# Reordering the start of a vision tower and the turn of its last image

## The chip, the cores and the metric

The kernel runs on one core of a Trainium2 chip. The metric is the device time of one execution, in microseconds (us); the kernel before has a median of 746.74 us over three runs (746.47 to 747.71). One further execution was recorded by the hardware profiler, and every row of a profile below is from such an execution. Engines are named as the profile names them: PE (matrix multiplication), DVE (VectorE), ACT (ScalarE), POOL (GpSimd) and SP (which here only starts transfers). Each engine runs its own queue of instructions in order and waits on semaphores for the others.

## The reference, cut to what matters

Four images of 3 x 224 x 224 pixels go through a tokenizer and two layers, all in float32. The tokenizer normalises 8 x 8 patches (192 values), multiplies them by `W1`, normalises, multiplies by `Wp1`, normalises, applies SiLU and multiplies by `Wp2`:

```python
tokens = layernorm(patches, ln1_g, ln1_b) @ W1 + b1
tokens = layernorm(tokens, ln2_g, ln2_b)
tokens = jnp.concatenate([tokens, tokens, tokens], axis=1)
h1 = silu(layernorm(tokens @ Wp1 + bp1, lnp_g, lnp_b))
return h1 @ Wp2 + bp2
```

Layer 0 is an attention *between the images* at each place, with a gate, and a mixture of six experts of which each token takes two:

```python
att = softmax(einsum('slhc,tlhc->sth', q, k) * scale, axis=1)
o = einsum('sth,tlhc->slhc', att, v) * sigmoid(mn @ Wg + bg)
...
top_w, top_i = top_k(softmax(relu(x @ router_w1 + b) @ router_w2 + b), 2)
out = sum over the two chosen experts of weight * expert(x)
```

Layer 1 is a linear attention and a small mixture of four experts. Tokens are repeated three times, so only a third of the rows is computed and the result is written three times.

## The kernel before, in words

Each image has 784 rows: six tiles of 128 rows and 16 rows left over; the leftovers of the four images share one more tile.

**Start.** SP and ACT issue the loads of the first weights and of the pixels (nine transfers into `img`). POOL issues the bias `bp1` and thirteen small vectors into `stage` (46 rows of 128 values) early. `first_layers` (L361) folds the first weight matrices into `Wall`; it is a generator whose parts are interleaved by hand with the pixels' work: `flatten(k)` (L341) copies the pixels of a seventh of the patches into rows, on DVE or ACT; `turn_patches(k, c)` (L349) transposes four columns of patches on PE (`ptp`) and copies them out to `pT`; `patch_stats` and `patch_stds` (L446, L451) find the standard deviations. At the end `stage` is transposed on PE to the columns `cols` (L525, L526). Large buffers in DRAM, `xrows` and `yrows`, are cleared by 46 transfers from a tile of zeros, `nothing`, behind that last copy. POOL also fills constant tables (`base0`, `table`, `blk`, `shift`).

**Middle.** `tokenize` works through groups of tiles; its order is left to the scheduler. From `turn_second(0)` on, the order of PE, DVE and ACT is written by hand (`tc.manual_schedule`): what stands earlier in the code stands earlier in each engine's queue. Keys and values of all images are computed (`keys_values`), and then each image s takes its turn (`added_rows`, `weighed`): `products` (DVE) multiplies queries with the keys of each image, `shares_before` and `shares_after` make the softmax `att`, `gate_mm` and `gate_act` the gate, `first_value` and `values` the weighted sum `oT`, `attended` multiplies by `Wo` (`pwo`), adds to `h` and takes the sums of squares, `rows_of_part` normalises, `turn_part` transposes (`pt`) to `xT`, `router` (`pr`, `rT`) and `router_logits` (`plg`) make the router's logits, `choose` (18 small DVE instructions) picks two experts, `count` (`pcount`) numbers the rows, and `send` computes their places and has POOL scatter them to `xrows`, one transfer for each tile and choice.

**Expert blocks.** Rows are handled in blocks of 256 of one expert. `early_blocks` (L1171) makes the list of the first seven blocks from the first two images, in three steps that alternate PE and DVE. A block is loaded by SP (`load`), transposed on PE (`turned`: `ptb`, `xTb`), its expert's weights are copied to one place by DVE (`own_weights`, which first reads the expert's offset from the list into a register), and then multiplied three times (`hidden(i, 0)`, `hidden(i, 1)`: `pb`, `hb`; `rows_back`: `pyb`, `yb`). The last image's turn (L1517 on) is interleaved by hand with the first blocks. All the experts' weights, `ew`, take the place of the keys and queries, `kq`, and are loaded by six transfers of SP once the last product has been taken; the loads of the first four blocks stand behind these on SP.

After the blocks, layer 1 follows; the change does not touch it.

Of the kernel before, what the change touches and what calls it, by code (L numbers as in the profile page):

```python
# [27 lines left out]
P = 128  # L28
TT = 128
# [43 lines left out]
def tile_vit_tower(ctx: ExitStack, tc: tile.TileContext, a: dict, out: bass.AP):  # L73
# [97 lines left out]
    img = tokp.tile([IP, CY, WID], F32, tag="img", name="img")  # L171
    bp1 = tokp.tile([TT, D], F32, tag="bp1", name="bp1")
    nc.gpsimd.dma_start(out=bp1, in_=a["L0_tok_bp1"].partition_broadcast(TT))
# [3 lines left out]
    for src, n, width in plan:  # L177
        nc.gpsimd.dma_start(out=stage[r0 : r0 + n, :width], in_=src)
        r0 += n
# [154 lines left out]
    pL = tokp.tile([P, 2, NI, SEG], F32, tag="pL", name="pL")  # L334
    nc.gpsimd.memset(pL, 1.0)
# [4 lines left out]

    def flatten(k, put):  # L341
        put(
            flat[:, k * PW : (k + 1) * PW, :PD].rearrange("q w (y x) -> q w y x", x=PATCH),
            img[:, :, k * PW * PATCH : (k + 1) * PW * PATCH].rearrange(
                "q y (w x) -> q w y x", x=PATCH
            ),
        )

# [12 lines left out]
    def first_layers():  # L361
# [68 lines left out]
        nc.vector.tensor_copy(Wall[:, :, D:], pp)  # L430
# [41 lines left out]
    with tc.manual_schedule(engines=by_hand):  # L472
        nc.vector.memset(srow, 0.0)
        nc.vector.memset(srow[:, SROW : SROW + 1], 1.0)
        nc.vector.memset(perm, 0.0)
        nc.vector.memset(perm[:, :, :PD], -1.0 / PD)
        by_y = ident[:KP, :KP].rearrange("p (y x c) -> p c y x", x=PATCH, c=CH)
        for half in range(2):
            nc.vector.tensor_scalar(
                perm[:, half, :PD].rearrange("p (c y x) -> p c y x", c=CH, x=PATCH)[  # L480
                    :, :, 4 * half : 4 * (half + 1)
                ],
                by_y, -1.0 / PD, None, ALU.add,
            )
        nc.scalar.activation(root_, one_, AF.Sqrt, bias=one_)
        warm = ps_tile("pwarm")
        for _ in range(6):
            nc.tensor.transpose(warm[:, :P], ident, ident)
        steps = first_layers()
        next(steps)  # L490
        NK = HP // PW
        cut0 = 5
        flatten(0, nc.vector.tensor_copy)
        flatten(1, nc.scalar.copy)
        turn_patches(0, 0)
        for k in range(2):
            patch_stats(k)
        flatten(3, nc.vector.tensor_copy)
        flatten(2, nc.scalar.copy)
        turn_patches(1, 0)  # L500
        next(steps)
        for k in range(2, cut0):
            patch_stats(k)
        turn_patches(2, 0)
        flatten(4, nc.scalar.copy)
        next(steps)
        turn_patches(3, 0)
        flatten(5, nc.scalar.copy)
        turn_patches(4, 0)
        patch_stds(0, cut0)  # L510
        turn_patches(5, 0)
        flatten(6, nc.scalar.copy)
        for k in range(2):
            turn_patches(k, 1)
        turn_patches(6, 0)
        for k in range(cut0, NK):
            patch_stats(k)
        for k in range(2, cut0):
            turn_patches(k, 1)
        patch_stds(cut0, NK)  # L520
        next(steps)
        turn_patches(5, 1)
        turn_patches(6, 1, nc.vector.tensor_copy)
        pc = ps_tile("pc")
        nc.tensor.transpose(pc[:, :nrows], stage, ident[:nrows, :nrows])  # L525
        turned = nc.vector.tensor_copy(cols, pc[:, :nrows])  # L526

# [16 lines left out]
    rb2 = spread(wts, "rb2", a["L0_ffn_router_b2"])  # L544
    for put in weight_loads:
        tc.add_manual_dep(
            put.ins, arrived[0],
            mybir.DependencyInfo(mybir.DependencyClass.Sync, mybir.DependencyReason.DATA),
            reason="behind the images",
        )  # L550

    nothing = tokp.tile([P, 7 * D], F32, tag="nothing", name="nothing")
    nc.gpsimd.memset(nothing, 0.0)
    for r in range(0, XROWS, 7 * P):
        n = min(7, (XROWS - r) // P)
        for rows_ in (xrows, yrows):
            put = nc.sync.dma_start(
                out=rows_[r : r + n * P, :].rearrange("(p k) d -> p (k d)", k=n),
                in_=nothing[:, : n * D],
            )  # L560
            tc.add_manual_dep(
                put.ins, turned.ins.name,
                mybir.DependencyInfo(mybir.DependencyClass.Sync, mybir.DependencyReason.DATA),
                reason="later",
            )
# [7 lines left out]
    base0 = const.tile([TT, E0], F32, tag="base0", name="base0")  # L573
    for e in range(E0):
        nc.gpsimd.memset(base0[:, e : e + 1], float(CAP * e))


    NQ = QMAX * E0
    table = const.tile([1, 5, NQ], F32, tag="table", name="table")
    for q in range(QMAX):  # L580
        nc.gpsimd.memset(table[:, 0, q * E0 : (q + 1) * E0], float(BLK * q))
    by_e = table.rearrange("r k (q e) -> r k q e", e=E0)
    for e in range(E0):
        for k, v in (
            (1, CAP * e - DUMMY), (2, EW * e), (3, D * e), (4, CAP * e - DUMMY + SMALL)
        ):
            nc.gpsimd.memset(by_e[:, k, :, e], float(v))
    for k in (1, 4):
        nc.gpsimd.tensor_tensor(table[:, k, :], table[:, 0, :], table[:, k, :], ALU.add)
    blk = const.tile([NQ, NBLK], F32, tag="blk", name="blk")  # L590
    for i in range(NBLK):
        nc.gpsimd.memset(blk[:, i : i + 1], float(i))
    shift = const.tile([1, 3, NBLK], F32, tag="shift", name="shift")
    nc.gpsimd.memset(shift, 0.0)
    nc.gpsimd.memset(shift[:, 0, :], float(DUMMY))
# [108 lines left out]
    for g in range(n - 1):  # L704
        if g == n - 2:
            second_rows(0, second_norm(0))
        tokenize(g)
# [121 lines left out]
    kq = keys.tile([P, 2 * TOK + 4 * SEQ], F32, tag="kq", name="kq")  # L829
    kT = kq[:, : 2 * TOK].rearrange("p (c n) -> p c n", c=2)  # L830
# [114 lines left out]
    def attended(s, two):  # L945
# [17 lines left out]
        nc.vector.tensor_scalar(part, part, -1.0 / D, None, ALU.mult)  # L963
        for j in two:
            nc.scalar.activation(
                junk, h[:, s * TPI + j, :], AF.Square, bias=nm[:, j : j + 1],
                accum_out=ss[:, j : j + 1],
            )
# [185 lines left out]
    def meta_of(these, place, n):  # L1154
# [7 lines left out]
        meta = small.tile([1, 3, n], I32, tag=f"meta{n}", name="meta", bufs=1)  # L1162
# [3 lines left out]
        return meta  # L1166

# [3 lines left out]
    def early_blocks():  # L1171
# [7 lines left out]
        place = numbered(full)  # L1179
        yield  # L1180
        nc.vector.tensor_scalar(taken, place, float(NEARLY), full, ALU.is_lt, ALU.mult)
        metas[0] = meta_of(full, place, NEARLY)
# [156 lines left out]

    def added_rows(s):  # L1340
# [3 lines left out]
        if s > 1:  # L1344
            products(s, 0, [NI - 1])
            choose(past)
# [47 lines left out]
    with tc.manual_schedule(engines=by_hand):  # L1394
# [125 lines left out]
    with tc.manual_schedule(engines=by_hand):  # L1520
        products(s, 1, [1])
        scales_of(u)
# [3 lines left out]
        gate_mm(s, 0)  # L1526
        shifts_of(u)
        products(s, 1, [2])
        next(steps)
        products(s, 1, [3])  # L1530
        next(steps)
        gate_act(s, 0)
        mx = shares_before(s)
        gate_mm(s, 1)
        for _ in steps:
            pass
# [4 lines left out]
    ew = keys.tile([P, E0, EW], F32, tag="kq", name="ew")  # L1541
    ewf[0] = ew.rearrange("p e n -> p (e n)")
# [4 lines left out]
    with tc.manual_schedule(engines=by_hand | {ENG.SP}):  # L1547
        for i, name in enumerate(("expert_w1", "expert_w2", "expert_w3")):
            for c in range(2):
                nc.sync.dma_start(  # L1550
                    out=ew[:, :, (2 * i + c) * D : (2 * i + c + 1) * D],
                    in_=a[f"L0_ffn_{name}"].rearrange("e (c p) n -> c p e n", p=P)[c],
                )
        for i in range(4):
            load(i)
# [4 lines left out]
        values(s, 0, 0, GN)  # L1560
        values(s, 1, 0, GN)
        turn_part(u)
        mix2(past)
        for o in range(2):
            first_value(s, o, *rest, nc.scalar)
        values(s, 0, *rest, range(1, 3))
# [3 lines left out]
        mix3(past)  # L1570
        values(s, 1, *rest)
        keep_left(s)
        router(u)
        scales_of(ua)
        router_logits(u)
        attended(s, [4, 5])
        shifts_of(ua)
        rows_of_part(ua)
        attended(s, [6])
        for i in (0, 1):  # L1580
            b = cols[:, rows[f"eb{i + 1}_0"] :][:, : 2 * E0].rearrange("p (e r) -> p e r", r=2)
            nc.vector.tensor_copy(ew[:, :, 6 * D + 2 * i : 6 * D + 2 * i + 2], b)
        choose(u)
        turned(0)
        turn_part(ua)
        own_weights(0)
        scales_of(ub)
        count(u)
        hidden(0, 0)
        shifts_of(ub)  # L1590
        rows_of_part(ub, both=True)
        own_weights(1)
        turned(1)
        router(ua)
        send(u)
# [811 lines left out]
```

## Time and profile before

| what | value |
|---|---|
| median of the runs | 746.74 us |
| the profiled execution's own time | 774.73 us |
| its span, from first to last instruction | 773.0 us |
| PE busy | 702.5 us (91% of the span) |
| DVE busy | 475.7 us (62%) |
| ACT busy | 333.9 us (43%) |
| POOL busy | 126.2 us (16%) |
| granted PE clock, mean | 0.967 |

The profiled execution is 28 us longer than the median of the runs without a profile, so its rows have to be scaled by 746.74/774.73 = 0.964 on the mean. A busy PE is not a PE at its peak: its matmuls are pipelined and their ends are modelled[...]. The places that the change touches lie at 0 to 36 us (the start) and at 229 to 300 us (the turn of the last image).

### The profile page before, as it was taken

The numbers are of one execution on the slowest core, as the hardware profiler recorded it, in microseconds if no ns is written. First come the engines' busy times: TensorE is split into PE (matmuls) and PEld (weight loads), VectorE is DVE, ScalarE is ACT, GpSimd is POOL, SyncE is SP. The second block draws the span as 40 slices with busy tenths as digits, with TensorE's granted clock in tenths as the row PEclk, the third lists the DMA queues.
The fourth block names the chain that finished last, engine by engine and source line by source line (L and its number), as shares of the span: only waits on it lengthen the run. The fifth ranks groups of instructions, "written<-read, shape, count | busy, mean of one in ns | idle before, by whom it ended". The sixth has DMA issues, their size and how long they took to land.

```text
span 773.0 us, 9815 instructions
## 1 busy us (share of the span) xinstructions
PE 702.5 (91%) x3005; PEld 479.4 (62%) x3005; DVE 475.7 (62%) x1487; ACT 333.9 (43%) x794; POOL 126.2 (16%) x232
## 2 busy tenths in 40 slices
PE   6889889999977778998899998789999999999996
PEld 4546555666655566787788874547776765554553
DVE  5686785869987553456444767348986844444541
ACT  1565766556674552342222326325446422222221
POOL 7200000000074226400003026724000000000000
PEclk9999999999998889999999998879999999999999
DMA  5799997000022913422324252312000012322333
GB/s 177 232 426 424 426 424 312 1 0 1 0 82 90 376 72 117 136 82 77 95 90 123 96 158 69 96 34 70 7 0 1 5 27 94 97 60 89 106 113 106
DMA packets 56284, 96.49 MB, mean 125 GB/s; under 512 B 6504, under 2 KB 46158, under 8 KB 56232
## 3 DMA queue, kind: packets, MB, share of 16 engines
q1 hardware_dynamic: 49732, 79.68, 28.8%
q0 software_dynamic: 5600, 14.32, 6.1%
q10 hardware_dynamic: 900, 1.86, 0.8%
q8 instruction: 24, 0.39, 0.2%
q14 instruction: 28, 0.23, 0.1%
HBM read 30.75 MB, written 65.09 MB: 124 GB/s over the span
## 4 chain that ended last, share of the span: by engine, by line
PE 68%; DVE 17%; ACT 7%; issue 4%; DMA 2%; DVEq 1%; another core or an unknown queue 1%; ACTq 0%
PE pb L1482 11%; PE pe L280 6%; PE pyb L1500 5%; PE ps L280 4%; PE pqk L1948 4%; PE pkv L280 4%; PE pt L271 4%; PE pw L622 3%; PE ps L2357 3%; PE pwp L291 3%; PE pukx L2047 3%; PE pout L2127 3%; DVE oT L930 3%; PE pout L2132 3%; DMA img<-in_x_dram 2%
## 5 line engine op out<-in xcount | busy, mean ns | idle before, releaser
L1121 POOL DMA_INDIRECT xrows<-xn,pos x50 | 53.0, 1061 | 246.4 <-DVE nm L980 189.4
L1705 POOL DMA_INDIRECT ys<-yrows,pos x50 | 49.1, 982 | 160.4 <-DMA yrows<-yb 126.7
L1482 PE MATMUL pb<-xTb,own 128*128 128x256 f32 (+1 forms) x240 | 55.8, 378 | 11.7 <-DVE own L1458 6.9
L1488 ACT ACTIVATE hb<-pb,own 128x256 f32<-128x256 f32 (+1 forms) x74 | 33.6, 457 | 62.6 <-PE pb L1482 51.3
L1948 PE MATMUL pqk<-Wqkv,lxT 128*128 128x512 f32 x100 | 49.9, 646 | 6.6 <-issue 6.6
L1482 PEld LDWEIGHTS pb<-xTb,own 128*128 128x128 f32 x240 | 42.3, 197 | 20.1 <-ACT hb L1488 7.8
L1500 PE MATMUL pyb<-own,hb 128*128 128x256 f32 x216 | 52.7, 384 | 0.3 <-ACT hb L1488 0.2
L1482 PE MATMUL pb<-hb,own 128*128 128x256 f32 (+1 forms) x240 | 52.1, 359 | 0.9 <-DVE hb L1490 0.6
L280 PE MATMUL pe<-xT,eW 128*128 128x512 f32 (+1 forms) x112 | 46.0, 553 | 0.0
L1500 PEld LDWEIGHTS pyb<-own,hb 128*128 128x128 f32 x216 | 40.8, 193 | 6.6 <-ACT hb L1488 0.6
L1482 PEld LDWEIGHTS pb<-hb,own 128*128 128x128 f32 x240 | 40.6, 190 | 5.8 <-DVE hb L1490 1.0
L1506 DVE TENSOR_TENSOR yb<-pyb,eb 128x512 f32<-128x512 f32 (+1 forms) x30 | 19.1, 638 | 39.1 <-PE pyb L1500 26.5
L622 PE MATMUL pw<-Wall,pT 128*128 128x512 f32 (+1 forms) x96 | 42.7, 593 | 0.0
L1471 ACT COPY xTb<-ptb 128x512 f32<-128x512 f32 (+1 forms) x30 | 16.2, 542 | 59.3 <-PE ptb L1467 49.3
L271 PE MATMUL pt<-ident,xn 128*128 128x128 f32 x200 | 30.4, 284 | 10.6 <-DVE xn L648 6.5
L271 PEld LDWEIGHTS pt<-ident,xn 128*128 128x128 f32 x200 | 23.8, 143 | 25.4 <-issue 6.2
L1490 DVE TENSOR_SCALAR hb<-pb,own 128x256 f32<-128x256 f32 (+1 forms) x46 | 20.5, 446 | 28.7 <-PE pb L1482 19.6
L1948 PEld LDWEIGHTS pqk<-Wqkv,lxT 128*128 128x128 f32 x100 | 19.9, 207 | 28.6 <-issue 26.8
L884 DVE SCALAR_TENSOR_TENSOR prod<-kq 128x784 f32<-128x784 f32 x32 | 30.4, 970 | 6.1 <-ACT kq L1298 3.4
L280 PEld LDWEIGHTS pe<-xT,eW 128*128 128x128 f32 x112 | 20.2, 190 | 21.6 <-issue 16.5
L1458 DVE COPY own<-ew 128x1540 f32 x30 | 28.9, 965 | 7.0 <-issue 2.6
L622 PEld LDWEIGHTS pw<-Wall,pT 128*128 128x128 f32 (+1 forms) x96 | 17.9, 189 | 20.0 <-issue 17.9
(420 smaller groups left out, 1469.1 us busy)
## 6 DMA issues: line engine op xcount, KB each, us to landing
xrows<-nothing SPq DMA_DIRECT2D x22, 896.0 KB
yrows<-nothing SPq DMA_DIRECT2D x22, 896.0 KB
out_dram<-h SPq DMA_DIRECT2D x23, 384.0 KB
xb<-xrows SPq DMA_DIRECT2D x24, 256.0 KB
yrows<-yb SPq DMA_DIRECT2D x24, 256.0 KB
ew<-in_L_ffn_expert_w_dram SPq DMA_DIRECT2D x6, 768.0 KB
wb<-wd SPq DMA_DIRECT2D x16, 128.0 KB
img<-in_x_dram SPq DMA_DIRECT2D x5, 294.0 KB
```

The lines of the kernel that those rows point to most:

```text
L271: nc.tensor.transpose(pt[:, j * TT : (j + 1) * TT], xn[:, j, c * P : (c + 1) * P], ident[:TT, :TT])
L280: nc.tensor.matmul(pm[: wcols.stop - wcols.start, :n], w[:, c, wcols], xT(c), start=(c == 0), stop=(c == chunks - 1),)
L291: nc.tensor.matmul(pm[:, i, :], xT(c, t), w[:, c, :], start=(c == 0), stop=(c == chunks - 1))
L622: nc.tensor.matmul(pm, pixels(c, tiles[j]), Wall[: K1[c], c, :], start=(c == 0), stop=(c == 1))
L884: nc.vector.scalar_tensor_tensor(prod, qTs[s][:, o, :], 1.0, kT[:, o, t * SEQ : (t + 1) * SEQ], ALU.mult, ALU.mult, accum_out=atts[s][:, o ...
L1121: put = nc.gpsimd.indirect_dma_start(out=xrows[:, :], out_offset=bass.IndirectOffsetOnAxis(ap=pos[:, k, t0 + j : t0 + j + 1], axis=0), in_ ...
L1458: nc.vector.tensor_copy(w, ewf[0][:, bass.ds(off, EW)])
L1482: nc.tensor.matmul(pm, wm[:, c, o * P : (o + 1) * P], src[:, c, :], start=(c == 0), stop=(c == 1),)
L1488: nc.scalar.activation(dst[:, o, :], pm, AF.Relu, bias=b)
L1500: nc.tensor.matmul(pm[:, t, :], src[:, c, t * P : (t + 1) * P], wm[:, c, :], start=(c == 0), stop=(c == 1),)
L1705: got = nc.gpsimd.indirect_dma_start(out=y[:, j, k, :], out_offset=None, in_=yrows[:, :], in_offset=bass.IndirectOffsetOnAxis(ap=pos[:, k, ...
L1948: nc.tensor.matmul(pqk, xTs[u][:, c, cut(j, 1)], Wqkv[:, c, : 2 * D], start=(c == 0), stop=(c == 1),)
```

## The change

Start:
- POOL makes `nothing`, `base0`, the tables and `pL` before it issues the small vectors. The transfers of `bp1` and of the thirteen vectors wait for the last of the flatten copies on DVE.
- DVE takes the flatten copies 0, 3 and 5 (before: 0 and 3). `WcT` is made before the pixels' work, eight more transposes of the identity (`warm`) stand behind it on PE, the copy of the second half of `Wall` goes from DVE to ACT, and the last `pT` copy from DVE to ACT. The first transposes (c = 0) of all seven pieces now come before all second ones.
- The columns `cols` are made later, in the group loop (behind the third tile of the first group on PE). The clearing transfers wait for the last patch statistics only.

Last image:
- The block list has five steps instead of three.
- Both gates' multiplications come first, one behind the other. `router(u)` and its relu move ahead of `attended`; `choose(u)` moves behind `attended`, the first two `own_weights` and `hidden(0, 0)`; `turned(0)` moves into `attended(s, [4, 5])`.
- The experts' weights are loaded expert by expert, 18 transfers of 256 KB, into the parts of `kq` whose last reader is done: experts 0 and 1 already in `added_rows(3)`, 2 behind the first product, 3 to 5 behind the last. The block loads stand behind the list's fifth step.

```diff
@@ start, POOL @@
+    nothing = tokp.tile([P, 7 * D], F32, tag="nothing", name="nothing")
+    nc.gpsimd.memset(nothing, 0.0)
+    base0 = ...   # and table, blk, shift, pL: moved here from below
-    nc.gpsimd.dma_start(out=bp1, in_=a["L0_tok_bp1"].partition_broadcast(TT))
+    small_loads.append(
+        nc.gpsimd.dma_start(out=bp1, in_=a["L0_tok_bp1"].partition_broadcast(TT))
+    )
...
-        nc.gpsimd.dma_start(out=stage[r0 : r0 + n, :width], in_=src)
+        small_loads.append(nc.gpsimd.dma_start(out=stage[r0 : r0 + n, :width], in_=src))
...
+    for put in small_loads:
+        tc.add_manual_dep(put.ins, flattened[-1], ..., reason="behind the copies")
...
-                put.ins, turned.ins.name,
+                put.ins, arrived[-1],
@@ first_layers @@
-        nc.vector.tensor_copy(Wall[:, :, D:], pp)
+        nc.scalar.copy(Wall[:, :, D:], pp)
+        yield
@@ pixels @@
+        next(steps)
+        for _ in range(8):
+            nc.tensor.transpose(warm[:, :P], ident, ident)
         flatten(0, nc.vector.tensor_copy)
         flatten(1, nc.scalar.copy)
         turn_patches(0, 0)
         for k in range(2):
             patch_stats(k)
-        flatten(3, nc.vector.tensor_copy)
         flatten(2, nc.scalar.copy)
         turn_patches(1, 0)
+        for k in (3, 5):
+            flatten(k, nc.vector.tensor_copy)
         next(steps)
         for k in range(2, cut0):
             patch_stats(k)
         turn_patches(2, 0)
         flatten(4, nc.scalar.copy)
+        turn_patches(3, 0)
+        flatten(6, nc.scalar.copy)
+        for k in range(4, NK):
+            turn_patches(k, 0)
         next(steps)
...
         patch_stds(0, cut0)
-        for k in range(2):
+        for k in range(cut0):
             turn_patches(k, 1)
...
         for k in range(cut0, NK):
             patch_stats(k)
+        next(steps)
+        patch_stds(cut0, NK)
+        for k in range(cut0, NK):
             turn_patches(k, 1)
-        pc = ps_tile("pc")
...
@@ group loop @@
+        if g == 1:
+            pc = ps_tile("pc")
+            nc.tensor.transpose(pc[:, :nrows], stage, ident[:nrows, :nrows])
+            nc.vector.tensor_copy(cols, pc[:, :nrows])
@@ early_blocks: a yield between the place's multiplication and its copy, and between pmeta and meta @@
@@ added_rows @@
             products(s, 0, [NI - 1])
+            if s == NI - 1:
+                expert_weights(range(2))
             choose(past)
@@ last image @@
+        gate_mm(s, 0)
+        gate_mm(s, 1)
         products(s, 1, [1])
+        expert_weights([2])
         scales_of(u)
         send(past)
         steps = early_blocks()
         next(steps)
-        gate_mm(s, 0)
         shifts_of(u)
         products(s, 1, [2])
         next(steps)
+        gate_act(s, 0)
         products(s, 1, [3])
+        expert_weights(range(3, E0))
         next(steps)
-        gate_act(s, 0)
         mx = shares_before(s)
-        gate_mm(s, 1)
-        for _ in steps:
-            pass
+        next(steps)
         gate_act(s, 1)
         shares_after(s, mx)
...
-        for i in range(4):
-            load(i)
         first_value(s, 0, 0, GN, nc.vector)
         first_value(s, 1, 0, GN, nc.scalar)
         rows_of_part(u)
         mix1(past)
         values(s, 0, 0, GN)
+        for _ in steps:
+            pass
+        for i in range(4):
+            load(i)
         values(s, 1, 0, GN)
         turn_part(u)
         mix2(past)
         for o in range(2):
             first_value(s, o, *rest, nc.scalar)
+        router(u)
         values(s, 0, *rest, range(1, 3))
         attended(s, [0, 1])
         values(s, 0, *rest, range(3, NI))
         attended(s, [2, 3])
         mix3(past)
+        scales_of(ua)
         values(s, 1, *rest)
         keep_left(s)
-        router(u)
-        scales_of(ua)
         router_logits(u)
-        attended(s, [4, 5])
         shifts_of(ua)
-        rows_of_part(ua)
-        attended(s, [6])
         for i in (0, 1):
...
             nc.vector.tensor_copy(ew[:, :, 6 * D + 2 * i : 6 * D + 2 * i + 2], b)
+        attended(s, [4, 5], 0)
+        own_weights(0)
+        rows_of_part(ua)
+        attended(s, [6])
+        hidden(0, 0)
+        turn_part(ua)
+        own_weights(1)
+        scales_of(ub)
         choose(u)
-        turned(0)
-        turn_part(ua)
-        own_weights(0)
-        scales_of(ub)
-        count(u)
-        hidden(0, 0)
+        turned(1)
         shifts_of(ub)
         rows_of_part(ub, both=True)
-        own_weights(1)
-        turned(1)
         router(ua)
+        count(u)
         send(u)
         hidden(0, 1)
```

The new helper that it calls:

```python
def expert_weights(es):
    for e in es:
        for i, name in enumerate(("expert_w1", "expert_w2", "expert_w3")):
            nc.sync.dma_start(
                out=ew[:, e, 2 * i * D : 2 * (i + 1) * D].rearrange("p (c n) -> p c n", c=2),
                in_=a[f"L0_ffn_{name}"][e].rearrange("(c p) n -> p c n", p=P),
            )
```

## The prediction

> **What bounds the kernel now.** I read the head of the page and the chain first (is PE the bound?), then the busy time by stage, then PE's waits in the stage that the change reorders, then the engines' timelines there and at the start.
>
> The head, and the chain's shares by engine:
>
> ```profile
> span 773.0 us, 9815 instructions
> ...
> PE 68%; DVE 17%; ACT 7%; issue 4%; DMA 2%; DVEq 1%; another core or an unknown queue 1%; ACTq 0%
> ```
>
> PE sets the end over most of the span, so the order of the other engines is worth something only where PE idles or runs slow. Where is that? The stages (stretch, length, then busy us of PE, PEld, DVE, ACT, POOL, granted PE clock, DMA share, GB/s):
>
> ```profile
> 31.50:236.80 205.30, 191.19 (x699) 118.62 (x697) 158.09 (x510) 127.28 (x249) 13.67 (x12) 0.98 0.51 210
> 236.80:251.50 14.70, 9.73 (x30) 5.57 (x29) 9.46 (x34) 7.29 (x17) 8.48 (x9) 0.77 0.37 125
> 251.50:278.90 27.40, 18.22 (x80) 13.84 (x79) 16.02 (x64) 16.12 (x41) 4.75 (x5) 0.85 0.82 288
> 278.90:300.60 21.70, 18.13 (x76) 13.98 (x76) 7.72 (x30) 6.54 (x14) 12.26 (x12) 0.88 0.29 97
> 300.60:773.00 472.40, 442.35 (x2028) 311.31 (x2028) 263.75 (x765) 164.22 (x452) 67.97 (x73) 0.97 0.25 77
> ```
>
> The last image's turn, 236.8 to 300.6, is the poor stretch: PE idles 17.7 of 63.8 us, at a lower clock. PE's waits at 229 to 300 us (who waited for whom: us, times, longest):
>
> ```profile
> PE plg L1030 <- ACT rT L1019: 3.9, 1, 3.9
> PE ptotal L1141 <- DVE often L1139: 3.2, 1, 3.2
> PE pt L271 <- ACT xn L995: 2.0, 4, 1.5
> PE pb L1482 <- DVE r L979: 1.8, 1, 1.8
> PE pmeta L1159 <- issue: 1.5, 1, 1.5
> ```
>
> These are the waits that the new order is placed against. What follows an idle stretch is slow: in PE's timeline the gates take 4.35 and 4.32 us, while the chain has as many matmuls of this form (`pq`) at 5.27 for twice the number, 2.64 each.
>
> ```profile
> 240.35 4.35 PE L280 MATMUL pg<-mT,Wg 128*128 128x392 f32 x8
> 247.23 4.32 PE L280 MATMUL pg<-mT,Wg 128*128 128x392 f32 x8
> ```
>
> At the start, all waits for the pixels until 16.60, and PE's first big multiplication starts at 30.87. DVE's two flatten copies have one form but 0.61 and 2.02 us; the slow one ran beside POOL's small memsets. POOL's small loads are slow too: it waited for `bp1`, issued at 4.29, until 12.62.
>
> ```profile
> 16.60 0.83 ACT L342 COPY vT<-img 126x768 f32<-126x768 f32 x1 [9.58 <-DMA img<-in_x_dram]
> L342 DVE COPY vT<-img x2: 614/1316/2019, 16.7 to 19.3; 126x768 f32<-126x768 f32 x2
> POOL stage L178 <- DMA bp<-in_L_tok_bp_dram: 2.8, 1, 2.8
> 30.87 5.43 PE L622 MATMUL pw<-Wall,pT 128*128 128x512 f32 x12
> ```
>
> [...] 3.25 us of idling before 240.1 and 3.9 before 265.16 are followed by a clock of 0.67 and 0.50. [...] 128 KB took over 7 us beside the pixels.
>
> **The last image, step by step.** Profile times; PE is at `pcount`'s end, 236.85, in both.
>
> 1. Gates first. Before: idle 3.25, then 4.35 and 4.32. Now 16 matmuls start at 236.85 with a warm PE: 5.3, to 242.1 (before: 251.5). Behind them stand `ptotal` and the list.
> 2. The added cost: DVE's `full` waits for `ptotal` behind both gates, until 242.5 (before 241.9). Queued behind it is the last product (0.97), so `pl` starts at 243.8. Two reductions, `exp`, and three more small ones give `att` at 245.7; before 248.63. Saved 3.0; the list's copies now fill `exp`'s wait.
> 3. ACT: gate 0's two halves run before `exp`, gate 1's after it (to 246.1), first value 0.65, six rows at 0.51: 249.8 (before 254.6). Mixing, then four `xT` copies: 252.0.
> 4. `router(u)` follows at once: `pr` from 251.2. PE was sparse for nine us, so I take half rate for most: 4.2 (warm 2.74), to 255.4. The relu now runs before the squares, ready by 256; the 3.9 us wait of `plg` is gone. `pwo` of four tiles at 1.74 a pair: 258.9.
> 5. DVE: values done at 252.2; sums of the first pair at 257.1 to 258; one product and gate 0.93; second pair to 259.9; mix 0.6; values 2.0 to 262.5 (before 265.66). `pwo` [4, 5] starts at 262.6 (before 267.74).
> 6. Sums to 265.5; the register read and its gap 1.1 (as before at 277.78), `own` 0.96: 267.6. Before, `choose(u)` (18 instructions, 3.64) stood ahead of it. The first expert matmul `pb` starts at **267.7, before 278.89: 11.2 earlier**.
> 7. Is its data there? Scatters of image 1 still start at 240.6 and POOL needs 12 x 1.27 = 15.2 us, so they land near 259; experts 3 to 5 (2.3 MB) are issued from 243.7 and take some 7 us at the 376 GB/s seen there. The first block load is issued at about 259 (before 262.04), lands before 263.
>
> Some of the 11.2 is not the order's. ACT's second `xT` copy waited until 257.83 for transposes that ended at 255.23, and the same sort of lag of about 2 us recurs at 294.2, 295.7 and 300.0. I suppose that it can recur, and take 2.3 off: 9 left.
>
> Then some is given back. `choose(u)` now runs at 269.9 to 273.6, ahead of `pcount`, `send(u)` and `hidden(0, 1)`; each of the 7 early blocks is as long as before. Following PE's new order from 267.7 (`pb` 3.7 cold, transposes 1.7, `pr` with its copies 2.4, `pcount` 0.9, `pb` 1.7, 0.8, 0.9, 1.7, `pyb` 1.8, `pr` 1.3, 0.4, `pb` 1.8) PE ends at 286.8; `choose(ua)`, 3.6 behind `yb`, holds `pcount` until 287.7, and the third block starts at 288.2. The same sum for the old order, without the lags, gives 295.1 (measured 300.64). So 7 to 9 remain, and I take **8.0**. POOL's chain does not eat it: `send(u)` at about 276 instead of 281.9, then 26 x 1.27 = 33 us, to 309 and landed by 311; block 7's load came at 328.54, so it would be wanted at 320. The last 470 us shift as they stand.
>
> **The start, step by step.** Less traffic beside the pixels: 128 KB of `bp1` and 24 of vectors out of some 3.1 MB at about 285 GB/s, 0.5 us, so pixels at 16.1. But what stands before them grows. Some 80 memsets now run at 4 to 11 us beside DVE's scaling of W1 (two at 0.36); by the 2.02 against 0.61 above it slips 0.8 (none to 1.5). PE's preamble ended at 14.74, now 15.6. On it follow four transposes (1.06) and eight `warm` ones: 0.26 each as at 2.60, or 0.13 each as the warm `ptp`: 1 to 2. So the first `ptp` starts at 18.5, not 17.33, and ACT's first `pT` copy at 19.3, not 18.47. From there ACT was busy or waiting 13.05 us to the end of the pixels' work. Now: flatten 3 x 0.73, fourteen copies at 0.46 (0.43 to 0.53), `Wall` 0.5, two roots at 0.33, and the waits: 1.0 for `pw`, and 0.73 behind each root, where before other copies covered one: 12.3. That ends at 31.6 against 31.5: **0.1 lost** (1.0 gained to 1.5 lost). DVE's third flatten costs 0.6 where DVE isn't last. The `cols` transpose, 0.26, moves behind twelve matmuls, under PE's same work. Clearing starts at about 26.3, not 31.59; nothing reads it before 220.
>
> **Sum.** -8.0 + 0.1 = -7.9 us against the profiled 774.73; scaled by 746.74/774.73, -7.6: **739.1 us**.
>
> **The rivals.**
>
> *A warm PE.* If PE's clock stays up at 251 (1.5), at `pb` (3.75 against 1.73: 2.0) and the lags don't recur, the gain is 11 to 13: 734.5. For it: the idle stretches shrink to about 2 us, below those that a low clock followed. Against: PE is thin between 243 and 251.
>
> *Given back downstream.* The new order has `choose(u)`, `own` and `send` compete on DVE with blocks 0 and 1, and lags take more; only 2 to 4 remain: 743.5. For it: PE waited at 295 to 300 for `choose(ua)` and would again.
>
> *Late vectors, slower than before.* The thirteen loads of `stage` start at 21 us, eight in flight, and the last five meet the clearing transfers that start at 26.3 (896 KB each, DMA share 1.00). `pc` stands on PE behind the twelfth matmul, at about 36.3, and each us that it waits is lost. If these loads take as long as under the pixels (8 us), they land at 35 to 37: a loss of 0 to 1. For the whole gain to go they must land after 44, so take over 15 us each: a backlog of eight clearings, 7.2 MB at 418 GB/s, is 17. For it: `bp1`'s wait is as long as draining the 2.1 MB outstanding at its issue. Against: the clearings have only just begun. At 17 us: 750.
>
> *No effect.* The two order changes are real in the queues, so this would be a balance of the above.
>
> **How the numbers follow.** The likeliest (0.55) has 736.5 to 742. The warm PE has 0.17, given back 0.18, late vectors 0.10. The range 733.5 to 745.5 holds the first three but their tails, and leaves the last out. By 0.2% (1.5 us), about what a measurement can tell: faster all of the first two, and 0.16 of the third: 0.88; within: 0.04; slower 0.08.
>
> **What would show it.** Right: both `pg` groups together at about 2.7 us each with no wait for `ptotal` ahead; no wait of `plg` for `rT`; the first `pb` 8 to 12 us earlier than the first `pw` moved; three flatten copies near 0.6. Wrong: PE waiting at `pc` or DVE at `bp1`; a first `pw` after 32.5; POOL's last scatter later than block 7's load; a low clock through 243 to 290.

## The result, and the profile after

The changed kernel takes **751.84 us** (median of 4 runs, 751.11 to 751.96); the kernel before takes 746.61 beside it (4 runs). The ratio is 1.0068, with a 95% interval of 1.0051 to 1.0086: slower by 5.2 us, where 7.6 us faster was forecast.

The runs were made on at least three chips: on two of them, chips 8 and 12 (here the *stalling* chips), the kernel before takes 764 to 777 us, and on chip 3 (the *quiet* chip) and in this first comparison, whose chip is not on record, 743 to 748. The first profile of before (774.73 us) has the length of a stalling chip, the profile of after (751.96 us) that of the quiet one. Up to the gates of the last image, at 236 us, the two can be compared line by line: the kernel with the turn alone, profiled on both kinds, has 148.1 and 147.95 us from its first `pw` to its first `pwo`, and 57.8 us on both from there to the gates. Behind that, profiles of the stalling chips show engines idle at some places with nothing that the profile shows to wait for (14.57 us at the longest in the turn alone on chip 8).

The head of the page and the chain's shares by engine, after:

```profile
span 750.0 us, 9854 instructions
...
PE 53%; DVE 6%; ACT 2%; issue 1%; DMA 1%; DVEq 1%; SPq 0%; ACTq 0%
```

These shares add up to 64% and not to 100: the chain is followed back only to 269.8 us, so it says nothing of what comes before.

The work of the last image's turn begins 14.2 us later than before, so the stretch of 63.8 us that the prediction called poor has to be taken from 251.0 on. First the prediction's first stage and then that stretch, both after; then the same stretch of a kernel with the old turn on the quiet chip ("The start alone", below; of before itself there is no profile from that chip). The columns are stretch, length, busy us of PE, PEld, DVE, ACT and POOL, granted PE clock, DMA share and GB/s:

```profile
31.50:236.80 205.30, 185.21 (x658) 112.39 (x656) 145.71 (x467) 122.20 (x237) 7.99 (x8) 0.96 0.49 201
251.00:314.80 63.80, 55.90 (x266) 44.09 (x266) 41.22 (x155) 36.53 (x86) 32.38 (x32) 0.92 0.57 190
```

```profile
240.00:303.80 63.80, 51.92 (x222) 38.89 (x222) 36.78 (x139) 33.07 (x79) 29.69 (x29) 0.87 0.56 197
```

The poor stretch has filled up, as it should: PE is busy 55.9 of its 63.8 us, where the profile of before has 46.1. But the old turn on the quiet chip has 51.9, so more than half of that difference is the chip's and not the order's. And in the first row, which the prediction had passed over as untouched, PE is busy 6.0 us less (185.21 against 191.19). PE's waits between 31 and 150 us say where; first after, then before (who waited for whom: us, times, longest):

```profile
PE pkv L310 <- ACT kq L1328: 9.7, 1, 9.7
PE pt L301 <- DVE xn L658: 6.4, 4, 2.8
```

```profile
PE pt L271 <- DVE xn L648: 6.5, 5, 2.8
PE pwp L291 <- ACT xTt L660: 0.8, 1, 0.8
```

The first row of after has no counterpart. PE waits 9.7 us for ACT to empty the keys' accumulators. And what does ACT wait for? Its timeline in after:

```profile
116.09 0.30 ACT L282 ACTIVATE v<-v,eps 128x3 f32<-128x3 f32 x1 [0.64 <-DVE v L281]
129.34 0.48 ACT L1326 COPY kq<-pkv 128x384 f32<-128x384 f32 x1 [12.95 <-DMA yrows<-nothing]
129.71 0.22 ACT L1328 COPY kq<-pkv 128x64 f32<-128x64 f32 x1
```

The same copy before does not wait:

```profile
112.89 0.46 ACT L1298 COPY kq<-pkv 128x384 f32<-128x384 f32 x1
```

The first copy of the keys waits 12.95 us for a *clearing transfer*. No data pass between the two: the keys' tile `kq` has taken over the memory of `nothing`, so its first write has to wait until the last transfer has read the zeros. In the built program `kq` lies at bytes 56384 to 94016 of each partition. `nothing` lay at 126464 to 133632 before, where no other tile is put until the expert blocks; it lies at 84288 to 91456 now, because it is allocated ahead of most tiles of its pool. The view of that tile (issues of the transfers, and who waited), after and before:

```profile
L590 SPq DMA_DIRECT2D yrows<-nothing x23: 332/332/1507, 26.8 to 113.7; - x23
...
  ACT kq L1326: 13.0, 1
```

```profile
L557 SPq DMA_DIRECT2D yrows<-nothing x23: 332/332/1837, 32.0 to 117.0; - x23
```

Before, the last transfer was issued even later, and nobody waited for it.

The last image's turn, by contrast, looks as forecast. After, PE's waits from 229 to 300 us begin, and the gates stand together:

```profile
PE pr L310 <- ACT xT L1026: 2.8, 1, 2.8
PE pb L1520 <- DVE own L1496: 2.4, 1, 2.4
PE pwo L321 <- DVE oT L950: 1.8, 1, 1.8
```

```profile
251.03 5.51 PE L310 MATMUL pg<-mT,Wg 128*128 128x392 f32 x16
256.38 0.24 PE L1158 MATMUL ptotal<-ones,often 128*78 128x1 f32 x2
```

The waits of `plg` (3.9) and `ptotal` (3.2) are gone, and both gates take 2.75 us each. At the start there is a new wait, of DVE for `bp1`, and the first big multiplication is later:

```profile
29.21 0.42 DVE L474 TENSOR_TENSOR bp<-pbw,bp 128x256 f32<-128x256 f32 x1 [1.92 <-DMA bp<-in_L_tok_bp_dram]
```

```profile
32.79 6.54 PE L632 MATMUL pw<-Wall,pT 128*128 128x512 f32 x12
```

So there were three terms to settle: the memory's wait, the start, and the turn.

### The profile page after: what moved, and what is told of

It is laid out like the page before. It is cut to its first block, busy times and chain, and to the rows that moved or that the text cites. A ratio compares the mean times of both kernels' runs of the same rounds, so it can differ in the third digit from the quotient of the medians.

```text
span 750.0 us, 9854 instructions
## 1 busy us (share of the span) xinstructions
PE 691.9 (92%) x3013; PEld 475.2 (63%) x3013; DVE 475.7 (63%) x1486; ACT 333.7 (45%) x795; POOL 125.6 (17%) x232
## 4 chain that ended last, share of the span: by engine, by line
PE 53%; DVE 6%; ACT 2%; issue 1%; DMA 1%; DVEq 1%; SPq 0%; ACTq 0%
PE pb L1520 12%; PE pe L310 6%; PE pyb L1538 5%; PE ps L310 4%; PE pqk L1981 4%; PE ps L2390 3%; PE pout L2160 3%; PE pout L2165 3%; PE pukx L2080 2%; PE pt L301 2%; PE pe L2360 2%; PE ps L2384 2%; PE ptb L1505 1%; DVE own L1496 1%; PE pkvo L2140 1%
## 5 line engine op out<-in xcount | busy, mean ns | idle before, releaser
L1981 PE MATMUL pqk<-Wqkv,lxT 128*128 128x512 f32 x100 | 44.9, 594 | 0.2 <-ACT lxT L94 0.2
L1544 DVE TENSOR_TENSOR yb<-pyb,eb 128x512 f32<-128x512 f32 (+1 forms) x30 | 19.1, 637 | 33.9 <-PE pyb L1538 33.5
L1496 DVE COPY own<-kq 128x1540 f32 x30 | 28.8, 963 | 7.9 <-ACT xTb L1509 2.4
L310 PE MATMUL pkv<-mT,Wv 128*128 128x384 f32 (+1 forms) x64 | 24.9, 531 | 9.7 <-ACT kq L1328 9.7
```

The costliest lines, as they stand in the source:

```text
L310: nc.tensor.matmul(pm[: wcols.stop - wcols.start, :n], w[:, c, wcols], xT(c), start=(c == 0), stop=(c == chunks - 1),)
L1496: nc.vector.tensor_copy(w, ewf[0][:, bass.ds(off, EW)])
L1981: nc.tensor.matmul(pqk, xTs[u][:, c, cut(j, 1)], Wqkv[:, c, : 2 * D], start=(c == 0), stop=(c == 1),)
```

## The experiments

Every kernel here computes the whole reference. "Marks" are starts in PE's timeline: the first `pw`, the first `pkv` (keys), the first `pwo`, and the first `pb` of a block. Theory A puts the loss on the wait of `kq`; rivals B and C on the start, and on a turn that gains nothing.

### The kernel before, profiled again

> The kernel before, unchanged, profiled a second time. Its first profiled execution took 774.73 us, 28 us over the median without a profile. If those 28 us were of that execution alone, this one takes 746 to 748 us, and the stretches that were long in the first (450 to 550 us, and the lags of 2 us at 257.8, 294, 296 and 300) are short here. If a profile costs this kernel 28 us each time, it takes about 774 again, and the profile of the changed kernel (751.96 us, no longer than its other runs) would hide a kernel that is 20 us faster, which its runs deny.

No edit. On chip 8 it took 772.69 us; 39 runs of before beside it have a median of 770.76 (765.52 to 776.81). So the 28 us belong neither to one execution nor to profiling; they go with the chip: chips 8 and 12 gave medians of 770.76 and 770.7 for this kernel, chip 3 gave 745.62 and 745.51. Its marks lie within 0.1 us of the first profile's at `pkv` (108.49 and 108.58) and `pwo` (178.78 and 178.88), though its pixels arrive 1.0 us sooner and its first `pw` starts 0.4 us sooner.

### The zeros placed elsewhere

```diff
     img = tokp.tile(...)
+    pT = tokp.tile(...)        # and the other tiles of the pool,
+    Wall = tokp.tile(...)      # allocated here in place of further down
+    ...
     nothing = tokp.tile([P, 7 * D], F32, tag="nothing", name="nothing")
```

No instruction is added, removed or moved; only addresses differ (`nothing` at 126176), and with them the waits.

> The changed kernel with its instructions and their order as they are; only the tile of zeros is given memory behind the other tiles of its pool, where neither the keys and queries nor the rows beside them take its place. Theory A (the loss is the first copy of the keys, which waits 13.0 us for the clearing transfers to be done with the memory that it takes over): that wait is gone, the 14.4 us of lag at 136 us fall back to the 3.4 that the start has, and the time is 738 to 743 us. Rival B (the loss is in the start and in what the clearing transfers do to the other transfers): the wait turns up at another place, 748 to 752 us. Rival C (the last image's turn gains nothing): the wait goes, but the time is 744 to 748.

On chip 8, where before takes 770.76, it took 771.26 (ratio 0.999, 0.9969 to 1.0011). The wait was gone, and the first `pwo` came at 182.37 in place of 193.24:

```profile
116.39 0.46 ACT L1326 COPY kq<-pkv 128x384 f32<-128x384 f32 x1
```

The end told nothing there: engines stood idle at 285 to 310 us with their input ready, so B and C were not yet out.

> The changed kernel, unchanged, beside the next three and the kernel before on one chip. On the chip of the first comparison it was 5.2 us slower than before. Theory A: 4 to 7 us slower than before here too, with a wait of 12 to 15 us of the first copy of the keys. If this chip adds the stalls that the last three profiles showed at 285 to 315 us (engines that stand 8 to 15 us with their input ready), the turn's gain is eaten as well and it is 10 to 13 us slower.

> The changed kernel with the tile of zeros behind the other tiles, once more, now beside the changed kernel itself. Theory A: 10 to 11.5 us faster than the changed kernel: the 10.9 us by which its work is earlier from 193 us on (182.37 against 193.24), wherever it runs. Against before: 4.5 to 6.5 us faster on a chip without the stalls, level with it on one that has them. Rival B: less than 3 us faster than the changed kernel, because another wait takes the place.

On the quiet chip, side by side: the changed kernel 751.88 (ratio 1.0077, 1.0059 to 1.0094), the placed one **740.08** (0.9917, 0.9888 to 0.9947). That is 11.8 us for an address, a little over what A said (10 to 11.5), and B is out; so is C, since the placed kernel beats the kernel before. Its tile view now ends with no one waiting. Its time lies 1 us from the forecast of 739.1, but that is in part luck: before took 745.62 in this comparison and 746.74 in the prediction's, so the gain is 5.5 us where 7.6 was forecast.

### The same mistake put into the kernel before

```diff
     img = tokp.tile(...)
+    nothing = tokp.tile([P, 7 * D], F32, tag="nothing", name="nothing")
...
-    nothing = tokp.tile([P, 7 * D], F32, tag="nothing", name="nothing")
     nc.gpsimd.memset(nothing, 0.0)
```

> The kernel before with one line moved: the tile of zeros is allocated behind the pixels' tile, so that the keys and queries later take its memory; what is done and in what order stays. Theory A: the first copy of the keys, at some 113 us, waits for the last clearing transfer, which was issued at 117.0 and lands near 130: 12 to 17 us lost, 758 to 764 us. Rival B: where the tile lies makes no difference: 746 to 748.

On chip 8, 790.07 against 770.76: ratio 1.0244 (1.0183 to 1.0304), 14 to 23 us lost by one moved line. Its ACT timeline:

```profile
133.58 0.48 ACT L1298 COPY kq<-pkv 128x384 f32<-128x384 f32 x1 [21.22 <-DMA yrows<-nothing]
```

A holds; its size was put too low. The copy that waits for the last transfer starts at 133.58; the expectation had it land near 130, 13 us behind the 117.0 at which before issues it. In the changed kernel the copy starts at 129.34 for an issue at 113.7, 15.6 us later.

### The turn alone

The kernel before, with the second half of the change (from `keys` on) and nothing of the first.

> The kernel before with the last image's part of the change alone: the reordered turn, the list in five steps, the experts' weights expert by expert. The start and the tile of zeros stay as before. Theory A: the turn gains what the prediction said and a little more, 8 to 12 us: 735 to 739 us, and the first expert multiplication comes 11 us earlier. Rival C: the gain is given back in the blocks that follow: 743 to 747.

> The last image's part alone, once more. Theory A: its first expert multiplication is 10 us earlier than before (268.66 against 278.19 in the last pair), and on a chip without the stalls 8 to 10 us of that reach the end: 3.5 us faster than the kernel with the start as well. Rival C (given back downstream): 1 to 3 us faster than before on every chip.

On chip 8 769.35 (0.9978, 0.9955 to 1.0001), on the quiet chip **738.21** against 745.62 (0.9899, 0.9882 to 0.9916): 7.4 us gained. Why next to nothing on chip 8? The turn itself gains as much there (first `pb` at 268.66, before 278.19), but then two engines stand. ACT and DVE of that run:

```profile
293.37 0.47 ACT L1512 ACTIVATE hb<-pb,own 128x256 f32<-128x256 f32 x1 [7.95 <-remote]
305.42 0.59 ACT L1495 COPY xTb<-ptb 128x512 f32<-128x512 f32 x1 [8.78 <-remote]
303.90 0.69 DVE L1530 TENSOR_TENSOR yb<-pyb,eb 128x512 f32<-128x512 f32 x1 [14.57 <-remote]
```

The multiplication that this `yb` reads had ended at 289.52. On the quiet chip the same instruction of the same program waits 2.68 us. What the engines wait for on chip 8 is in no view. The kernel before stands there as well (in its second profile ACT 7.88 us ahead of the `xTb` copy at 313.06), so why such stalls take the turn's whole gain was not settled.

### The start alone

```diff
+    (first half of the change: POOL, vectors, copies, order of the pixels' work)
+    nothing allocated behind the other tiles
     (turn of the last image as before)
```

> The start's part alone, with the tile of zeros behind the other tiles; the last image's turn as before. Theory A: the start costs 3.2 to 3.7 us, as the marks at 112 and 182 us of the placed kernel say (3.5 later than before), and all of it reaches the end: 3 to 4 us slower than before. The prediction had 0.1 us here, with 1.5 as its worst. Rival: the start is level and the 3.5 us belong to the clearing transfers that begin earlier; then this kernel is also 3 to 4 slower, but its first multiplication of the pixels begins no later than before (30.9 us), and the lag grows between 40 and 112 us.

On the quiet chip, 748.57 against 745.62: ratio 1.0031 (1.0016 to 1.0045), **3.0 us lost**, where the prediction had 0.1. First `pw` at 32.77 (before 30.87), `pkv` at 111.91 (108.58), `pwo` at 182.20 (178.88). Over all profiles the first `pw` lies at 30.0 to 31.3 with the old start (nine) and at 31.6 to 33.9 with the new one (five). So 1.9 us are lost by 33 us, not after 40, and the rest soon after: the first twelve `pw` took 6.54 us in the profile of after, in place of 5.43, with PE's granted clock at 0.76 from 31 to 40 us (1.00 before); here they took 6.53.

This run has the old turn on the quiet chip, so it is the proper measure of the turn. Counted from the first `pwo`: the first `pb` 96.5 us later, the third block 114.5 and the span's end 564.8; in the placed kernel, which differs by the turn alone, 87.7, 106.1 and 557.1.

### bp1 alone, and POOL's whole order

```diff
+    nc.gpsimd.dma_start(out=bp1, in_=...)      # ahead of the zeros, no wait
     nc.gpsimd.memset(nothing, 0.0)
...
-    small_loads.append(nc.gpsimd.dma_start(out=bp1, in_=...))
```

> The placed kernel (both parts of the change, the tile of zeros behind the other tiles), and the load of bp1 issued early again, ahead of the zeros, as in the kernel before; the thirteen small vectors stay behind the copies. In the placed kernel DVE waited 2.06 us for bp1, and queued behind its addition stand the four small instructions of the second root. Theory A (the late bp1 is most of the start's loss): the wait is gone, the second root starts at 28.1 (ACT is free at 28.07) and not at 29.78, the first multiplication of the pixels at 31.1 and not at 32.8, and the time is 1.7 us under the placed kernel: 738.4 where that takes 740.1. Rival (PE's low clock is the loss, and the second root would be late anyhow): less than 0.5 us, 739.6 to 740.1.

> The placed kernel with bp1 loaded early, once more, to read its end. Its first profile showed the DVE's wait for bp1 gone, the first multiplication of the pixels 14.35 us behind DVE's first copy of pixels in place of 15.3 to 16.9, but PE standing 2.71 us at the transpose of the vectors, which land at 40. Theory A now: what the early bp1 gives is taken by the late vectors; within 1 us of the placed kernel, 739 to 741. Rival (the wait for the vectors is covered by what follows): 738 to 738.5.

No gain: 771.92 on chip 12 (ratio 1.0007, 0.9988 to 1.0027), 740.24 (0.9934, 0.9913 to 0.9955) on the quiet chip, where the placed kernel took 740.08. In the first profile the second root did start sooner (29.30, with ACT busy until then), and the first `pw` stood at 30.58. But PE then met what came next, which the later `pw` had covered:

```profile
40.35 0.23 PE L717 MATMUL pc<-ident,stage 46*128 46x46 f32 x1 [2.71 <-issue]
```

The vectors, issued from 24.7 on, were not there. In the second profile the pixels came later, the first `pw` stood at 32.83, and `pc` still waited 1.46 us. One thing did come back in both: the first twelve `pw` take 5.35 us (before: 5.43). In all five profiles with a late `bp1` they take 6.36 to 6.59. The edit also moved the zeros' memset by 1.3 us, beside DVE's small copies: the two of `gbT` took 1.58 and 1.57 us in place of 0.16 and 0.15, and the `WcT` copy came at 17.67 in place of 16.42. So it is no clean test of `bp1` alone.

```diff
-    nothing, base0, table, blk, shift, pL made ahead of the vectors
+    nc.gpsimd.dma_start(out=bp1, in_=...)      # and the vectors: early, no wait
+    nothing, base0, table, blk, shift, pL where they were before
```

> Both parts of the change, but POOL's order as in the kernel before: bp1 and the vectors early and without a wait, the zeros and tables behind them (which puts the tile of zeros where it was before). PE's, DVE's and ACT's orders are those of the changed kernel. Theory A: both scalings of W1 take 0.73 again in place of 2.51, what hangs on them comes 0.8 sooner, and DVE does not wait for bp1: the first multiplication of the pixels starts at 30.0 to 30.6, and the time is 737.0 to 738.2, which is level with the kernel that has the turn alone (738.2) or a little better. Rival (the other changes of the start cost too: a cold PE, the copy of Wall on ACT): the first multiplication comes after 31, and it takes over 738.7.

> Both parts of the change with POOL's order as before, once more, to read its end. In its first profile the first multiplication of the pixels stood at 30.80 (14.56 us behind DVE's first copy of pixels; with the turn alone 14.1 to 14.3), and the keys' first multiplication at 108.60, as before. Theory A (all that the start costs is POOL's new order): 737.5 to 739, level with the turn alone (738.2). Rival (the other moves of the start gain by themselves): under 737.

769.05 on chip 12 (0.9987, 0.9967 to 1.0007) and, on the quiet chip, **736.04** against 745.51 (0.9894, 0.9856 to 0.9933). It beats the kernel before and the changed one, and can't be told apart from the turn alone, which was measured beside other runs (0.9899). One of its four runs took 740.45, so against the placed kernel (0.9917) the medians alone do not decide; the marks do: in its two profiles the first `pw` stands at 30.80 and 30.40 and `pkv` at 108.6 and 107.1, where the placed kernel has 31.58 to 32.85 and 110.7 to 112.1. The scaling of W1, in the placed kernel and here:

```profile
6.88 2.51 DVE L422 TENSOR_SCALAR W1g<-W,m,gbT 96x256 f32<-96x256 f32 x2
```

```profile
6.83 0.73 DVE L386 TENSOR_SCALAR W1g<-W,m,gbT 96x256 f32<-96x256 f32 x2
```

So POOL's new order accounts for the start's loss; the reordered pixels' work, the `Wall` copy on ACT and the third flatten on DVE neither gain nor lose what these runs can tell. Nor is it the earlier clearing, which waits for the last patch statistics here too: they end at 26.34 in the first of these profiles, and at 26.33 in after, where the clearing begins at 26.40. The edit puts back the memsets, `bp1` and the vectors at once, so how the loss divides among them is not shown.

### Two steps of the turn undone

Both in the kernel with the turn alone.

```diff
         attended(s, [4, 5], 0)
+        choose(u)
         own_weights(0)
...
-        choose(u)
         turned(1)
```

> The kernel with the turn alone, and in it one step undone: the 18 small instructions of the choice of experts for the second image but one stand ahead of the first block's weights again, as before. Theory A (step 6 of the prediction): the weights' copy and the first expert multiplication come 3.6 us later (272.3 in place of 268.7); since the choice then no longer holds up what follows, about half is got back by the third block, and the time is 2 us over the turn alone: 740.2. Rival (the same instructions have to be done before the count anyhow): level with the turn alone, 738.2.

> The turn alone with the choice of experts back ahead of the first block's weights, once more, to read its end. In its first profile PE waited 5.23 us for those weights, and the first expert multiplication came 94.7 us behind the first output projection, against 87.6 to 89.5 with the choice behind. Theory A (step 6): 2 to 5 us slower than the turn alone: 740.2 to 743. Rival: level, 738 to 739.

767.21 on chip 12 (0.9968, 0.9947 to 0.9989) and 740.36 on the quiet chip (0.9936, 0.9915 to 0.9956), there 2.2 us over the turn alone. PE's waits there begin with

```profile
PE pb L1506 <- DVE own L1482: 5.6, 1, 5.6
```

The first `pb` comes 3.5 us later (91.1 behind the first `pwo`, in place of 87.6), the third block 3.8. Theory A's 3.6 is right for the first; that half is got back by the third block is not, though the medians differ by 2.2 only.

```diff
-        gate_mm(s, 0)
-        gate_mm(s, 1)
         products(s, 1, [1])
...
         next(steps)
+        gate_mm(s, 0)
         shifts_of(u)
...
         mx = shares_before(s)
+        gate_mm(s, 1)
         next(steps)
```

> The kernel with the turn alone, and in it another step undone: the two gates' multiplications stand where they stood before, one behind the list's total, one behind the softmax's sums. Theory A (steps 1 to 3 of the prediction): PE idles 3.3 us ahead of the total again, each gate takes 4.3 us in place of 2.7, the second gate and with it the values come 3 to 4 us later, and the first expert multiplication as well: 741 to 742. Rival (the second gate is not what the values wait for): under 1 us, 738.2 to 739.

> The turn alone with the gates' multiplications back at their old places, once more, to read its end. In its first profile the first expert multiplication came 94.4 us behind the first output projection, against 87.6 to 89.5. Theory A (steps 1 to 3): 3 to 7 us slower than the turn alone: 741 to 745. Rival: what is late there is made up in the blocks, 738 to 739.5.

775.38 on chip 12 (1.005, 1.0022 to 1.0077) and 739.03 on the quiet chip (0.9907, 0.988 to 0.9934). On the quiet chip the rival wins: PE's wait for `ptotal` is back,

```profile
PE ptotal L1144 <- DVE often L1142: 3.8, 1, 3.8
```

but the first `pb` is 1.4 us later (89.0 behind `pwo`) and the third block 0.2. On chip 12 the profile shows the first `pb` 94.4 behind `pwo`, and the time is 6 to 8 us over two other kernels with the rest of the new turn on that chip (769.05 and 767.21). So there this order does cost; why was not found.

## Why the prediction was wrong

**The step that failed** is a term put at nothing, in the last sentence of the start: "Clearing starts at about 26.3, not 31.59; nothing reads it before 220." The start was right (26.4). But the question was put to the wrong tile: who reads what the transfers *write*, and not who takes the memory that they *read*. Moving the memset up also moved the allocation up, and so changed an address. What the prediction held at nothing costs 11.8 us, more than the whole gain. The added waits stood in the built program of the changed kernel: the first `kq` copy had gained a wait on every hardware DMA queue and on POOL. They were overlooked.

**The start**, "0.1 lost (1.0 gained to 1.5 lost)", measured 3.0. The slip of 0.8 by the memsets was right: DVE's two scalings of W1 took 2.51 in place of 0.73, and the copy into `Wall` 0.8 later, 13.56 against 12.76 (the placed kernel beside the turn alone). The 2.51 us, from 6.88 to 9.39, ran beside POOL's row of small memsets (6.53 to 9.2), and the 0.73, from 6.83 to 7.56, beside none; why the scalings are slow there is not shown.

Missing from the sum was `bp1`. The prediction named "DVE at `bp1`" as a sign of being wrong, but priced it only as traffic saved. Its addition stands ahead of the second root's input on DVE. Did its wait of 1.92 us reach the second root, which ACT takes? First the profile of after, then the placed kernel's second:

```profile
30.70 0.31 ACT L492 ACTIVATE vT<-pv,eps 126x8 f32<-126x8 f32 x1
```

```profile
29.78 0.31 ACT L498 ACTIVATE vT<-pv,eps 126x8 f32<-126x8 f32 x1 [1.71 <-DVE pv L497]
```

In after it did not: ACT was busy until 30.70 with the copies of slow transposes (twenty in 4.46 us). In the other profile the transposes ran fast (the last fifteen in 1.78 us), and ACT stood 1.71 us. So there were two obstacles in front of the second root, and each can hide the other; what each took of the 3.0 us is not shown. Also mis-sized: the `pT` copies behind the first root, taken at 0.46 and measured 0.84 apart in four of the five profiles, each waiting 0.31 for a slow transpose; and the twelve first `pw`, which were not expected to slow down and lost 1.1 us. "Pixels at 16.1" can't be judged: DVE's first copy of them starts at 16.82 in the first profile of after and at 15.64 to 17.99 in the other four, against 15.66 to 16.66 in profiles of the old start. The three flatten copies did take 0.56 and 1.08 for two, as forecast.

**The turn**, "I take 8.0": 7.4 by the medians, 8.5 at the third block, 8.9 at the first `pb` ("9 left"). By its own steps, in the run of the turn alone, moved by 0.87 to the prediction's clock: gates end 242.2 (242.1), `pl` 243.5 (243.8), `pr` from 250.1 for 4.49 (251.2, 4.2), `pwo` [4, 5] 261.6 (262.6), `pb` 266.5 (267.7). POOL's last scatter started at 309.2 on that clock in the placed kernel (forecast to 309). So the sum was right, yet one reason for it was not: steps 1 to 3, the gates first, bring under 1 us on the quiet chip and not 3, since the third block starts within 0.2 us without them. Step 6, the choice behind the first weights, brings 2.2 to 3.8. The rest lies in the moves that were not undone one by one (the router ahead of `attended`, the experts' weights in pieces, the list in five steps); it was not split further.

The three terms do not add up to the last us: 3.0 lost, 11.8 lost and 7.4 gained make 7.4 lost, and the changed kernel lost 5.2 and 6.3 in two comparisons; start and turn together gain 5.5 in the placed kernel where the single kernels give 4.4. The intervals, 1 to 2 us each way, cover this.

**The lags of 2 us** that the prediction supposed could recur, and for which it took 2.3 off, are absent on the quiet chip. With the old turn the first `pb` comes 96.5 us behind the first `pwo` there, and 100.0 in the profile that the prediction was worked out from. So 3.5 of its 11.2 us were the profile's, not the order's. Scaling all by 0.964 spread the chip's 28 us over the span, while they lie behind 236 us.

**The rivals.** *A warm PE*: not with the new turn on the quiet chip, where the first `pb` took 3.06 us (1.97 in the blocks behind it) and `pr` 4.49; and where it did take 1.97, in the kernel with the gates put back, the end was no earlier. *Given back downstream*: not on the quiet chip. *Late vectors*: not in the changed kernel, where `pc` at 40.98 did not wait; but only just, as the early `bp1` showed.

## What to carry to other kernels

A tile that is allocated earlier is also allocated elsewhere. When a change moves an allocation, list what will later lie over it and which transfers still read or write it then; a wait on many DMA queues, on an instruction that takes nothing from them, is the sign. And before costing a stretch from one profile, compare that execution with the kernel's ordinary time: here 28 us of it went with the chip, and made the stretch to be mended look poorer than it was.

## What was not expected of the hardware

- In the changed kernel a transfer issued at 113.7 had landed by 129.3 (15.6 us). At the 417 GB/s that the page of after shows up to 112 us, 15.6 us are some 6.5 MB, about seven of these transfers of 896 KB (an estimate from these numbers).
- Twenty transposes took 4.46 us in one execution of the placed kernel, and the last fifteen of them 1.78 us in the other (0.22 against 0.12 each); the first `pw` came 1.3 us sooner in the second.
- On chip 8, in the turn alone and in the placed kernel, the same two instructions stood with their input ready: a copy of ACT (`xTb`) 8.8 us and an addition of DVE (`yb`) 14.6 us. PE waited 6.4 us for that copy in both, and on chip 12, with the early `bp1` and with POOL's old order, 7.1 and 5.8 us. On chip 3 it does not wait there in any of the four. The kernel before takes 25 us more on chips 8 and 12; how much of that is such stalls was not worked out, and their cause stays open.
